# Label-major masks in a graph-attention kernel: contiguous ScalarE copies with strided sums for node tiles 0 and 1, a VectorE multiply-add chain for node tiles 2 and 3

## The chip, the cores and the metric

The kernel runs on one core of one Trainium2 chip. The metric is the device time of one execution in microseconds (us). The core has five engines that each work through a queue of their own in order: TensorE (PE in the profile, with its weight loads as PEld), VectorE (DVE), ScalarE (ACT), GpSimd (POOL) and SyncE (SP), which issues DMA transfers. They wait for each other through semaphores.

## The reference

There are 16 graphs (`B`), each with 512 nodes of 512 features and 11 integer edge labels between every pair of nodes. Two directions of attention are added to a linear layer; only the first 20 nodes are attended to. Cut to what matters here:

```python
adj_f = adj.astype(jnp.float32)                  # (16, 512, 512, 11), entries 0 or 1
self_feat = vcq @ W_self.T + b_self
output = self_feat
for d in range(2):
    A = adj_f if d == 0 else jnp.swapaxes(adj_f, 1, 2)
    A = A[:, :, :20, :]
    cond = A.sum(-1)                             # how many labels an edge has
    vb = A @ w_bias + b_bias                     # the bias of an edge from its labels
    # aff: (16, 512, 16 heads, 20)
    aff = jnp.where(cond[:, :, None, :] > 0, aff, NEG) + vb[:, :, None, :]
    w = jax.nn.softmax(aff, axis=-1)
    output = output + (w applied to the 20 nodes' features, then Wout, bout)
return v + jax.nn.relu(output)
```

The change touches how `cond` (the count over 11 labels) and `vb` (the weighted sum over 11 labels) are formed on the chip. The two together make one additive mask: `vb`, plus -9e15 where the count is zero.

## The kernel before, in words

**Tiling.** A node tile is 128 nodes on the 128 partitions; a graph has 4 of them (`nt` 0 to 3). For each node there are `S` = 40 mask entries (2 directions by 20 nodes) of `L` = 11 labels. Masks are made for two node tiles at a time: `h` = 0 is node tiles 0 and 1, `h` = 1 is node tiles 2 and 3. So one mask step works on 128 partitions by 80 entries by 11 labels = 880 integers, loaded by `load_adj` into `adjs[b, h]`.

**The mask steps.** `mask_mul(b, h)` makes the products label times weight in `prod`, 80 rows of 12 places: on ScalarE by 11 instructions, one per label, that read every 11th integer and write every 12th place (for graph 0 by one ScalarE copy and one GpSimd multiply). `mask_count(b, h)` sums the 11 labels of each entry on VectorE (L323) into `cond`, and GpSimd writes -9e15 or 0 into the 12th place of `prod` (L324). `mask_sum(b, h)` sums the 12 places on VectorE (L329) into `add`. `mask_spread` copies `add` on ScalarE into four partition groups (L338, 16 copies of 32 partitions), and `full_add` on GpSimd (L345) adds the scores' constant part; the result is `full`.

**The loop.** After a setup of some 90 us, each pass of the loop `for b` takes one graph through four node tiles, while the products of the next graph's linear layer are made (`product`, L284, in seven steps after Strassen) and the attention of the previous graph's values is applied (`attend`, L436). For each node tile PE makes the scores (L366); then VectorE does `weigh` (adds the mask L380, takes the maximum L384, subtracts it L388); ScalarE takes the exponential (L393, `expo`); VectorE sums it and takes the reciprocal (`normal`, L416, L417), GpSimd multiplies (L418), and VectorE transposes (`turn`, L425). The softmax of one node tile is finished during the next one.

**The order.** It is written out by hand: each engine's queue holds the instructions in the order of the code. In node tile 0 of graph b stand `mask_mul(b, 1)`, the half of the scores, `normal` of the node tile before, `partial(b, 1, 0)` (L290, which PE's second half of the scores needs), `mask_count(b, 1)`, `joined` (L300), `mask_sum(b, 1)`, half of `mask_spread(b, 1)`, `weigh`, `expo` and the other half. In node tile 2 stands `mask_mul(b + 1, 0)`. In node tile 3 stand `mask_count(b + 1, 0)`, `normal`, `mask_sum(b + 1, 0)`, all of `mask_spread(b + 1, 0)`, then `weigh` and `expo`. So on ScalarE the exponential of node tile 3 stands behind 16 copies that wait for `mask_sum(b + 1, 0)`. `partial(b, f, l)` and `joined(b, key, f, l)` read PE's product out of PSUM and free the bank for the next product. `load_adj(b + 1, 0)` is issued on SP behind `mask_sum(b, 1)` (`done["masks"]`).

Of the kernel before, what the change touches and what calls it, by code (L numbers as in the profile page):

```python
# [7 lines left out]
F32 = mybir.dt.float32  # L8
I32 = mybir.dt.int32
AF = mybir.ActivationFunctionType  # L10
ALU = mybir.AluOpType
AX = mybir.AxisListType

P = 128
NEG = -9000000000000000.0
# [3 lines left out]
def gat_kernel(  # L19
# [19 lines left out]
):  # L39
    nc = tc.nc  # L40
    B, F, N = xT.shape
    NG, L = adj.shape[3], adj.shape[4]
    H, DH = 16, 32
    C = F // P
    HL = P // DH
# [2 lines left out]
    S = 2 * NG  # L48
# [13 lines left out]
    msk = ctx.enter_context(tc.tile_pool(name="msk", bufs=2))  # L62
# [14 lines left out]
    wb_sb = const.tile([P, L], F32, name="wb_sb")  # L77
# [14 lines left out]
    xs, xns, rss, adjs, nzs, sfs, cqs, gs, vds = {}, {}, {}, {}, {}, {}, {}, {}, {}  # L92
    adds, fulls, wts, outs, held, conds, prods = {}, {}, {}, [], [None] * 3, {}, {}
    sums, parts, done, cleared = {}, {}, {}, []


    def behind(one, other):

        if other is not None:
            info = mybir.DependencyInfo(mybir.DependencyClass.Sync, mybir.DependencyReason.DATA)  # L100
            tc.add_manual_dep(one.ins, other.ins.name, info, reason="loads in turn")
# [13 lines left out]
    def load_adj(b, h, ins=None, ts=slice(0, 2)):  # L115
        if ts.start == 0:
            adjs[b, h] = load.tile([P, 2, S * L], I32, tag="adj", name=f"adj{b}_{h}", bufs=3)
        a = adj[b, h * 2 * P : (h + 1) * 2 * P].rearrange("(t p) d m l -> p t (d m l)", p=P)
        behind(nc.sync.dma_start(adjs[b, h][:, ts], a[:, ts]), ins)

    def load_cq(b, ins=None):
# [182 lines left out]
    def new_self(b):  # L304
        sfs[b] = sfp.tile([P, C, N], F32, tag="sf", name=f"sf{b}")
        nc.scalar.copy(sfs[b][:, :, :NG], kvn[:, :, bass.ts(b, NG)])

    def mask_mul(b, h):
        a = adjs[b, h].rearrange("p t (m l) -> p (t m) l", l=L)
        p = prods[b, h] = (msk if h == 0 or b == 0 else xsum).tile(  # L310
            [P, 2 * S, L + 1], F32, tag="prod", name=f"prod{b}_{h}", bufs=1
        )
        if b == 0:
            nc.scalar.copy(p[:, :, :L], a)
            nc.gpsimd.tensor_mul(p[:, :, :L], p[:, :, :L], wb_sb.unsqueeze(1).to_broadcast([P, 2 * S, L]))
        else:
            for l in range(L):
                nc.scalar.activation(p[:, :, l], a[:, :, l], AF.Identity, scale=wb_sb[:, l : l + 1])  # L318

    def mask_count(b, h):  # L320
        a = adjs[b, h]
        cond = msk.tile([P, 2 * S], F32, tag="cond", name=f"cond{b}_{h}")
        nc.vector.tensor_reduce(cond, a.rearrange("p t (m l) -> p (t m) l", l=L), AX.X, ALU.add)  # L323
        nc.gpsimd.tensor_scalar(prods[b, h][:, :, L], cond, 0.0, NEG, ALU.is_le, ALU.mult)  # L324

    def mask_sum(b, h):

        add = conds[b, h] = msk.tile([P, 2 * S], F32, tag="add", name=f"add{b}_{h}")
        done["masks"] = nc.vector.tensor_reduce(add, prods.pop((b, h)), AX.X, ALU.add)  # L329
        adds[b, h] = msk.tile([P, 2, HL, S], F32, tag="both", name=f"both{b}_{h}")  # L330

    def mask_spread(b, h, quarters=range(4)):
# [128 lines left out]
    with tc.tile_pool(name="setup", bufs=1) as sp, tc.tile_pool(name="ps_acc", bufs=4, space=PSUM) as acc["pool"]:  # L461
# [19 lines left out]
        with tc.tile_pool(name="setup_k", bufs=1) as sk:  # L481
# [41 lines left out]
            load_x(0)  # L523
            nc.sync.dma_start(wb_sb, w_bias.partition_broadcast(P))
            load_adj(0, 0)
            nc.sync.dma_start(bq_sb, bq)
            nc.sync.dma_start(bb_sb, b_bias.partition_broadcast(P))
            nc.sync.dma_start(bo_sb, bout)
            for d in range(2):
                rows(wo_sb[:, d], woT[d])  # L530
            load_x(1)
            load_adj(0, 1)


# [90 lines left out]
        with tc.tile_pool(name="setup_g", bufs=3) as sg:  # L625
# [131 lines left out]
            for n, runs in enumerate(bursts):  # L757
# [7 lines left out]
                if rest:  # L765
                    for kind in "mm" if n else ():
                        f, args = steps[kind].pop(0)
# [3 lines left out]
                for kind in plan[n - first] if n - first < len(plan) else ():  # L771
                    f, args = steps[kind].pop(0)
# [3 lines left out]
                if n == 7:  # L776
                    mask_mul(0, 0)
                if n == 8:
                    mask_count(0, 0)
                if n == 10:  # L780
                    mask_sum(0, 0)
                    load_cq(0)
# [13 lines left out]
                if n == 14:  # L796
                    mask_mul(0, 1)
                if n == 15:
                    mask_count(0, 1)
# [10 lines left out]
    with tc.manual_schedule():  # L810
# [10 lines left out]
        for b in range(B):  # L821
# [7 lines left out]
            for nt in range(NT):  # L829
# [13 lines left out]
                if nt == 0:  # L843
                    if b == 0:
                        for g in range(2):
                            scores(b, nt, g, ps[g])
                        mask_sum(b, 1)
                    else:
                        mask_mul(b, 1)
                        product(b, 4)  # L850
                        for g in range(2):
                            scores(b, nt, g, ps[g], range(2))
                        normal(*prev)
                        partial(b, 1, 0)
                        if more:
                            load_x(b + 1, range(2, 3), done["sum"])
                            load_x(b + 1, range(3, C), done["normal"])
                        for g in range(2):
                            scores(b, nt, g, ps[g], range(2, C))
                        if more:  # L860
                            row_mask(b + 1)
                        mask_count(b, 1)
                        joined(b, "c", 1, 1)
                        product(b, 3)
                        load_values(b - 1, done["joined"])
                        mask_sum(b, 1)
                        if more:
                            load_adj(b + 1, 0, done["masks"], slice(0, 1))
                        if b in (3, 4, 5):
                            copies = copies or blocks(1)  # L870
                            spill(1)
# [162 lines left out]
        b = B - 1  # L1034
# [77 lines left out]
```

## Time and profile before

| | |
|---|---|
| three runs | 580.94, 581.45, 582.77 us; median 581.45 us |
| the profiled execution's span, first to last instruction | 578.9 us |
| the median less that span (what lies around it) | 2.55 us |
| busy: PE, PEld, DVE, ACT, POOL | 99%, 75%, 85%, 68%, 70% |
| granted PE clock over the span | 0.998 |
| one pass of the loop in the steady state | 30.48 us |

No separate time is listed for the profiled execution; its span stands for it, and the difference to the median of the runs is kept as what lies around it. Lines of the profile give start, length, engine, line of the kernel, operation, output and inputs, and in brackets how long the engine sat idle before and whom it waited for. A group of several instructions ("x11") is given from the start of the first to the end of the last.

### The profile page before, as it was taken

To read this page: it belongs to the slowest core of one execution; us is meant where nothing else is said; L and a number is where in the kernel's file an instruction comes from. 1 tells how busy PE (TensorE), PEld (TensorE's weight loads), DVE (VectorE), ACT (ScalarE), POOL (GpSimd) and SP (SyncE) were. 2 spreads that over 40 slices of the span, in tenths; PEclk is the share of its full clock that TensorE was granted. 3 is DMA by queue.
4 is the path that set the end of the run, shared out by engine and by line. 5 is a ranking of instruction groups with operands and counts; after the bars stand their busy time and mean duration, and the time that the engine had idled before them with its cause. 6 is when DMAs were issued, how large, how long until landed. Compare 5 with 4: busy or idle time off the path is not lost.

```text
span 578.9 us, 31006 instructions
## 1 busy us (share of the span) xinstructions
PE 572.2 (99%) x13508; PEld 434.1 (75%) x13508; DVE 492.9 (85%) x790; ACT 393.6 (68%) x1162; POOL 404.6 (70%) x383
## 2 busy tenths in 40 slices
PE   9999999999999999999999999999999999999996
PEld 6544458888878787878778787877887878787873
DVE  0675776979898989898999999898989898989896
ACT  1234554687878777778786868687887877777571
POOL 2726986658586776858585867776858677785874
PEclk9999999999999999999999999999999999999999
DMA  8998997867777767777676777566666766674404
GB/s 315 382 396 283 333 361 233 237 195 219 209 233 185 220 187 204 213 185 228 167 220 166 222 166 220 164 206 180 204 193 192 195 192 189 192 208 111 147 19 147
DMA packets 98788, 123.26 MB, mean 213 GB/s; under 512 B 18877, under 2 KB 66969, under 8 KB 96605
## 3 DMA queue, kind: packets, MB, share of 16 engines
q1 hardware_dynamic: 96268, 117.54, 67.8%
q0 software_dynamic: 1392, 2.43, 1.8%
q8 instruction: 106, 1.74, 1.3%
q10 hardware_dynamic: 992, 1.31, 0.6%
q14 instruction: 30, 0.24, 0.1%
HBM read 82.30 MB, written 40.24 MB: 212 GB/s over the span
## 4 chain that ended last, share of the span: by engine, by line
PE 98%; DVE 1%; issue 0%; DVEq 0%
PE ps_s L366 46%; PE ps_a L284 19%; PE ps_c L284 9%; PE ps_o L436 6%; PE ps_d L284 5%; PE ps_v L658 3%; PE ps_k L598 3%; PE ps_kv L541 1%; PE ps_o L813 1%; PE ps_warm L500 1%; PE ps_nz L214 0%; PE ps_s L355 0%; PE _g(2, 2, 0, 14, 16)0_845 L692 0%; PE _g(0, 2, 0, 14, 16)0_448 L692 0%; PE g(3, 2, 0, 14, 16)0_1055 L692 0%
## 5 line engine op out<-in xcount | busy, mean ns | idle before, releaser
L366 PEld LDWEIGHTS ps_s<-g,sf 128*32 128x32 f32 x8192 | 263.6, 110 | 21.9 <-issue 14.8
L366 PE MATMUL ps_s<-g,sf 128*32 128x152 f32 x8192 | 278.1, 293 | 0.7 <-issue 0.7
L338 ACT COPY both<-add 32x80 f32<-32x80 f32 x512 | 130.9, 256 | 60.9 <-DVE add L329 55.1
L418 POOL TENSOR_TENSOR s<-s,sm 128x640 f32<-128x640 f32 x63 | 80.4, 1275 | 96.8 <-DVE sm L417 52.5
L345 POOL TENSOR_TENSOR full<-cq,both 128x640 f32<-128x640 f32 x64 | 100.3, 1568 | 26.9 <-issue 20.9
L318 ACT ACTIVATE prod<-adj,wb_sb 128x80 f32<-128x80 int32 x330 | 112.4, 432 | 0.0
L393 ACT ACTIVATE s<-s 128x640 f32<-128x640 f32 x63 | 46.5, 738 | 56.0 <-DVE s L388 55.6
L450 POOL TENSOR_TENSOR o<-o,x 128x512 f32<-128x512 f32 x60 | 76.3, 1293 | 0.0
L380 DVE TENSOR_TENSOR full<-ps_s,full 128x608 f32<-128x608 f32 x63 | 48.6, 772 | 22.5 <-PE ps_s L366 19.4
L284 PE MATMUL ps_a<-t,ws_s 128*32 128x246 f32 x1024 | 59.8, 371 | 0.0
L416 DVE TENSOR_REDUCE sm<-s 128x32 f32<-128x640 f32 x63 | 50.8, 807 | 10.5 <-ACT s L393 10.3
L384 DVE TENSOR_REDUCE ps_s<-full 128x32 f32<-128x640 f32 x63 | 52.2, 828 | 2.2
L425 DVE STREAM_TRANSPOSE wt<-s 128x640 f32<-128x640 f32 x63 | 52.8, 838 | 0.6 <-POOL s L418 0.6
L388 DVE TENSOR_TENSOR s<-full,ps_s 128x640 f32<-128x640 f32 x63 | 51.5, 818 | 1.1
L290 DVE SCALAR_TENSOR_TENSOR sf<-nz,qw,ps_a 128x246 f32<-128x246 f32 x128 | 51.5, 443 | 0.1
L284 PEld LDWEIGHTS ps_a<-t,ws_s 128*32 128x32 f32 x1024 | 34.4, 110 | 16.8 <-issue 0.8
L329 DVE TENSOR_REDUCE add<-prod 128x80 f32<-128x960 f32 x32 | 36.8, 1150 | 7.4 <-ACT prod L318 4.0
L447 ACT ACTIVATE o<-o,bo 128x512 f32<-128x512 f32 x60 | 38.3, 713 | 0.6 <-DVE o L445 0.6
L249 POOL TENSOR_TENSOR t<-x,t 128x492 f32<-128x492 f32 x32 | 36.8, 1151 | 1.3
L436 PE MATMUL ps_o<-wt,vd 32*32 32x512 f32 (+5 forms) x816 | 36.9, 578 | 0.0
L249 POOL TENSOR_TENSOR t<-x 128x492 f32<-128x492 f32 x32 | 36.8, 1151 | 0.0
L445 DVE TENSOR_TENSOR o<-ps_o,sf 128x512 f32<-128x512 f32 x60 | 36.7, 668 | 0.0
(225 smaller groups left out, 715.8 us busy)
## 6 DMA issues: line engine op xcount, KB each, us to landing
g<-g_d SPq DMA_DIRECT2D x60, 304.0 KB
g_d<-st SPq DMA_DIRECT2D x16, 1064.0 KB
out_T<-o SPq DMA_DIRECT2D x60, 256.0 KB
xn<-in_xn SPq DMA_DIRECT2D x56, 256.0 KB
x<-in_xT SPq DMA_DIRECT2D x56, 256.0 KB
adj<-in_adj SPq DMA_DIRECT2D x60, 220.0 KB
nz<-nz_d SPq DMA_DIRECT2D x14, 256.0 KB
wk<-in_wkT SPq DMA_DIRECT2D x2, 1024.0 KB
```

The costliest lines, as they stand in the source:

```text
L249: done["xsum"] = nc.gpsimd.tensor_sub(t, one, two)
L284: nc.tensor.matmul(to, lhs, x[:, k], start=start, stop=stop, skip_group_check=n != 2)
L290: done["partial"] = nc.vector.scalar_tensor_tensor(to[:, i], nzs[b][:, half(l)], qw[:, 2 * f + i, b : b + 1], parts[b, "a"][i][:, :HN], AL ...
L318: nc.scalar.activation(p[:, :, l], a[:, :, l], AF.Identity, scale=wb_sb[:, l : l + 1])
L338: done["spread"] = nc.scalar.copy(adds[b, h][bass.ts(a, R), :, g], add[r].rearrange("p (t m) -> p t m", t=2))
L345: done["full"] = nc.gpsimd.tensor_add(f, cqs[b].unsqueeze(1).to_broadcast(shape), adds[b, nt // 2][:, nt % 2].unsqueeze(2).to_broadcast(sh ...
L366: nc.tensor.matmul(to, sfs[b][:, k, bass.ds(nt * P + (2 * g + j) * R, R)], of, start=(onto is None and k == 0 and (whole or j == 0)), stop ...
L384: nc.vector.tensor_reduce(mx, f, AX.X, ALU.max)
L418: done["normal"] = nc.gpsimd.tensor_mul(s, s, sm.unsqueeze(3).to_broadcast(full))
L425: nc.vector.transpose(wts[b][:, nt], s.rearrange("p a h m -> p (a h m)"))
L436: nc.tensor.matmul(banks[a][bass.ds(at // 2 * DH, n * DH)].rearrange("p (t n) -> p t n", n=32), vd[r, bass.ds(at * DH, n * DH)], wt[r, :, ...
L450: nc.gpsimd.tensor_add(o[:, c], o[:, c], xs[b][:, c])
```

## The change

The integers come in label-major: for each node tile 11 runs of 40 entries in place of 40 runs of 11 labels. The host transposes them (outside the measured time), the bytes per transfer are the same. The product tile becomes 12 rows of 80 places.

- `mask_mul(b, 0)`: 11 ScalarE instructions as before, now with contiguous runs of 40 in and 80 out, for graph 0 too (its ScalarE copy and GpSimd multiply are gone).
- `mask_mul(b, 1)`: nothing is computed; only the tile is allocated.
- `mask_count(b, h)`: the same count on VectorE, but its 11 inputs for each entry stand 40 places apart. The GpSimd step writes a contiguous row.
- `mask_sum(b, 0)`: the same sum on VectorE, with its 12 inputs 80 places apart.
- `mask_sum(b, 1)`: in place of the sum, 11 VectorE multiply-adds of 80 elements, each adding label times weight to the result of the one before, starting from the -9e15 row.

```diff
     def mask_mul(b, h):
-        a = adjs[b, h].rearrange("p t (m l) -> p (t m) l", l=L)
         p = prods[b, h] = (msk if h == 0 or b == 0 else xsum).tile(
-            [P, 2 * S, L + 1], F32, tag="prod", name=f"prod{b}_{h}", bufs=1
+            [P, L + 1, 2 * S], F32, tag="prod", name=f"prod{b}_{h}", bufs=1
         )
-        if b == 0:
-            nc.scalar.copy(p[:, :, :L], a)
-            nc.gpsimd.tensor_mul(p[:, :, :L], p[:, :, :L], wb_sb.unsqueeze(1).to_broadcast([P, 2 * S, L]))
+        if h == 1:
+            return
+        for l in range(L):
+            nc.scalar.activation(
+                p[:, l].rearrange("p (t m) -> p t m", t=2), labels(b, h)[:, l], AF.Identity, scale=wb_sb[:, l : l + 1]
+            )
+    def labels(b, h):
+        return adjs[b, h].rearrange("p t (l m) -> p l t m", l=L)
...
+    def mask_count(b, h):
+        cond = msk.tile([P, 2, S], F32, tag="cond", name=f"cond{b}_{h}")
+        nc.vector.tensor_reduce(cond, labels(b, h).rearrange("p l t m -> p t m l"), AX.X, ALU.add)
+        nc.gpsimd.tensor_scalar(prods[b, h][:, L], cond.rearrange("p t m -> p (t m)"), 0.0, NEG, ALU.is_le, ALU.mult)
...
     def mask_sum(b, h):
+        if h == 0:
+            done["masks"] = nc.vector.tensor_reduce(add, p.rearrange("p l m -> p m l"), AX.X, ALU.add)
         else:
+            to = add.rearrange("p (t m) -> p t m", t=2)
             for l in range(L):
+                done["masks"] = nc.vector.scalar_tensor_tensor(
+                    to, labels(b, h)[:, l], wb_sb[:, l : l + 1],
+                    to if l else p[:, L].rearrange("p (t m) -> p t m", t=2), ALU.mult, ALU.add,
+                )
```

On VectorE in node tile 0 of a middle graph, before: the count (L323), `joined` (L300), the sum (L329), then `weigh` (L380 to L388).

```order
L323 TENSOR_REDUCE cond_1_4179<-adj_1_3646 128x80
L300 TENSOR_TENSOR sf_3889<-ps_c_4041,sf_3889 128x2x246
L329 TENSOR_REDUCE add_1_4204<-prod_1_4076 128x80
L380 TENSOR_TENSOR full_0_4073<-ps_s_0_4075,full_0_4073 128x32x19
L384 TENSOR_REDUCE ps_s_0_4075<-full_0_4073 128x32
L388 TENSOR_TENSOR s_0_4220<-full_0_4073,ps_s_0_4075 128x640
```

The same place now, with the line numbers of the changed kernel (L324 is the count, L336 the multiply-add, L390 to L398 `weigh`) and with the semaphores that each waits for:

```order
L324 TENSOR_REDUCE cond_1_4181<-adj_1_3659 128x80 [waits DMAHW7_49,DMAHW0_49]
L300 TENSOR_TENSOR sf_3902<-ps_c_4054,sf_3902 128x2x246
L336 SCALAR_TENSOR_TENSOR add_1_4206<-adj_1_3659,wb_sb,prod_1_4089 128x80 [waits Pool_49]
L336 SCALAR_TENSOR_TENSOR add_1_4206<-adj_1_3659,wb_sb,add_1_4206 128x80 [waits DVE_49] x10
L390 TENSOR_TENSOR full_0_4086<-ps_s_0_4088,full_0_4086 128x32x19 [waits PE_49]
```

One instruction became eleven, ten of which wait for the one before; the wait for ScalarE is gone, that for GpSimd stays.

On ScalarE from the masks of `h` = 0 of one graph to the second half of the copies of `h` = 1, before:

```order
L338 COPY both_0_2733<-add_0_2731 32x2x40 x16
L393 ACTIVATE s_3_2852<-s_3_2852 128x640
L318 ACTIVATE prod_1_2866<-adj_1_2437,wb_sb 128x80 x11
L338 COPY both_1_2996<-add_1_2994 32x2x40 x8
L393 ACTIVATE s_0_3010<-s_0_3010 128x640
```

The same place now (the copies are L348, the exponential is L403):

```order
L348 COPY both_0_2748<-add_0_2746 32x2x40 x16
L403 ACTIVATE s_3_2867<-s_3_2867 128x640
L348 COPY both_1_3010<-add_1_2998 32x2x40 x8
L403 ACTIVATE s_0_3024<-s_0_3024 128x640
L348 COPY both_1_3010<-add_1_2998 32x2x40 x8
```

The 11 products of `h` = 1 are gone from ScalarE; the order of what is left is the same, and the 16 copies still stand ahead of the exponential of node tile 3.

More of the change, by code (lines that the diff above doesn't have):

```diff
@@ L41, in gat_kernel @@
     B, F, N = xT.shape
-    NG, L = adj.shape[3], adj.shape[4]
+    L, NG = adj.shape[2], adj.shape[4]
     H, DH = 16, 32
@@ L117, in load_adj @@
             adjs[b, h] = load.tile([P, 2, S * L], I32, tag="adj", name=f"adj{b}_{h}", bufs=3)
-        a = adj[b, h * 2 * P : (h + 1) * 2 * P].rearrange("(t p) d m l -> p t (d m l)", p=P)
+        a = adj[b, h * 2 * P : (h + 1) * 2 * P].rearrange("(t p) l d m -> p t (l d m)", p=P)
         behind(nc.sync.dma_start(adjs[b, h][:, ts], a[:, ts]), ins)
@@ L306, in new_self @@
         nc.scalar.copy(sfs[b][:, :, :NG], kvn[:, :, bass.ts(b, NG)])
+    def labels(b, h):
+        return adjs[b, h].rearrange("p t (l m) -> p l t m", l=L)
     def mask_mul(b, h):
-        a = adjs[b, h].rearrange("p t (m l) -> p (t m) l", l=L)
         p = prods[b, h] = (msk if h == 0 or b == 0 else xsum).tile(
-            [P, 2 * S, L + 1], F32, tag="prod", name=f"prod{b}_{h}", bufs=1
+            [P, L + 1, 2 * S], F32, tag="prod", name=f"prod{b}_{h}", bufs=1
         )
-        if b == 0:
-            nc.scalar.copy(p[:, :, :L], a)
-            nc.gpsimd.tensor_mul(p[:, :, :L], p[:, :, :L], wb_sb.unsqueeze(1).to_broadcast([P, 2 * S, L]))
-        else:
-            for l in range(L):
-                nc.scalar.activation(p[:, :, l], a[:, :, l], AF.Identity, scale=wb_sb[:, l : l + 1])
+        if h == 1:
[4 more added lines that the diff above has]
+            )
@@ L320, in mask_count @@
     def mask_count(b, h):
[L321 to L324, printed above, removed]
+        cond = msk.tile([P, 2, S], F32, tag="cond", name=f"cond{b}_{h}")
+        nc.vector.tensor_reduce(cond, labels(b, h).rearrange("p l t m -> p t m l"), AX.X, ALU.add)
+        nc.gpsimd.tensor_scalar(prods[b, h][:, L], cond.rearrange("p t m -> p (t m)"), 0.0, NEG, ALU.is_le, ALU.mult)
@@ L326, in mask_sum @@
     def mask_sum(b, h):
         add = conds[b, h] = msk.tile([P, 2 * S], F32, tag="add", name=f"add{b}_{h}")
-        done["masks"] = nc.vector.tensor_reduce(add, prods.pop((b, h)), AX.X, ALU.add)
+        p = prods.pop((b, h))
+        if h == 0:
+            done["masks"] = nc.vector.tensor_reduce(add, p.rearrange("p l m -> p m l"), AX.X, ALU.add)
+        else:
+            to = add.rearrange("p (t m) -> p t m", t=2)
+            for l in range(L):
+                done["masks"] = nc.vector.scalar_tensor_tensor(
+                    to, labels(b, h)[:, l], wb_sb[:, l : l + 1],
+                    to if l else p[:, L].rearrange("p (t m) -> p t m", t=2), ALU.mult, ALU.add,
+                )
@@ L1087 @@
         "qT": chunked(given["cond_1024"]).transpose(0, 2, 1),
-        "adj": np.stack([mask[:, :, :NG], mask[:, :NG].transpose(0, 2, 1, 3)], axis=2),
+        "adj": np.stack([mask[:, :, :NG], mask[:, :NG].transpose(0, 2, 1, 3)], axis=2).transpose(0, 1, 4, 2, 3),
         "wsT": w["W_self"].T,
```

## The prediction

> **What bounds the kernel now.** I read the page first: who is busy, and what the chain that ended last consists of.
>
> ```profile
> span 578.9 us, 31006 instructions
> ...
> PE 572.2 (99%) x13508; PEld 434.1 (75%) x13508; DVE 492.9 (85%) x790; ACT 393.6 (68%) x1162; POOL 404.6 (70%) x383
> ...
> PE 98%; DVE 1%; issue 0%; DVEq 0%
> ```
>
> TensorE (PE) is busy for 572.2 of 578.9 us and makes up 98% of the chain: it is the bound, and nothing the change does makes PE's work shorter. The most that can be won is PE's idle 6.7 us. What can be lost depends on how much room VectorE (DVE) has, since the change gives it more work. So I took one pass of the loop in the middle by the busy-time windows (columns: length, busy PE, PEld, DVE, ACT, POOL, clock, DMA), from one sum L416 of node tile 3 to the next:
>
> ```profile
> 301.17:331.65 30.48, 30.48 (x792) 24.21 (x784) 27.83 (x43) 23.48 (x72) 22.04 (x20) 1.00 0.70 195
> ```
>
> PE fills the pass of 30.48 us without a gap; DVE has 2.65 us of it free. Where that freedom lies, DVE's timeline of the pass shows:
>
> ```profile
> 301.17 0.82 DVE L416 TENSOR_REDUCE sm<-s 128x32 f32<-128x640 f32 x1 [0.57 <-ACT s L393]
> 302.02 0.35 DVE L417 RECIPROCAL sm<-sm 128x32 f32<-128x32 f32 x1
> ...
> 302.96 1.06 DVE L323 TENSOR_REDUCE cond<-adj 128x80 f32<-128x880 int32 x1
> 303.94 0.66 DVE L300 TENSOR_TENSOR sf<-ps_c,sf 128x492 f32<-128x492 f32 x1
> 304.89 1.16 DVE L329 TENSOR_REDUCE add<-prod 128x80 f32<-128x960 f32 x1 [0.29 <-ACT prod L318]
> 305.96 0.78 DVE L380 TENSOR_TENSOR full<-ps_s,full 128x608 f32<-128x608 f32 x1
> ...
> 311.69 0.79 DVE L380 TENSOR_TENSOR full<-ps_s,full 128x608 f32<-128x608 f32 x1 [0.81 <-PE ps_s L366]
> ...
> 319.85 0.84 DVE L290 SCALAR_TENSOR_TENSOR sf<-nz,qw,ps_a 128x246 f32<-128x246 f32 x2
> ...
> 325.41 1.15 DVE L329 TENSOR_REDUCE add<-prod 128x80 f32<-128x960 f32 x1
> ...
> 331.65 0.82 DVE L416 TENSOR_REDUCE sm<-s 128x32 f32<-128x640 f32 x1 [0.58 <-ACT s L393]
> ```
>
> From the sum L416 at 301.17 to the end of the mask sum at 326.56 (25.39 us) DVE waits only twice: 0.29 and 0.81 us. What follows is not DVE's alone. ScalarE (ACT) makes 16 copies of that mask sum before it gets to the exponential that the next L416 needs:
>
> ```profile
> 326.59 4.27 ACT L338 COPY both<-add 32x80 f32<-32x80 f32 x16 [1.88 <-DVE add L329]
> 330.88 0.74 ACT L393 ACTIVATE s<-s 128x640 f32<-128x640 f32 x1
> ```
>
> So there is a ring in every pass: DVE from L416 to the mask sum, then 326.56 to 331.65 (5.09 us) on ACT, then L416 again. Without its two waits the ring takes 25.39 - 1.10 + 5.09 = 29.38 us against PE's 30.48. **The slack is 1.10 us per pass.** What DVE gets in addition beyond it lengthens each pass; the rest of DVE's free time lies beside the copies and the exponential on ACT and cannot be used. PE can't run ahead of this ring: its product behind the scores waits in every pass for DVE's L290 (319.85, done at 320.69), which stands between two of `weigh`'s steps, with only 0.44 us to spare:
>
> ```profile
> 321.13 1.85 PE L284 MATMUL ps_a<-t,ws_s 128*32 128x246 f32 x32
> ```
>
> **The change part by part.** The chain of multiply-adds. What it replaces takes 1.07 us in the order (304.89 to the next start at 305.96). For a scalar_tensor_tensor on data in SBUF the trace has one group:
>
> ```profile
> L611 DVE SCALAR_TENSOR_TENSOR bqt<-wq_sb,br_sb 128x512 f32<-128x512 f32 x8 | 5.4, 715 | 0.0
> L318 ACT ACTIVATE prod<-adj,wb_sb 128x80 f32<-128x80 int32 x330 | 112.4, 432 | 0.0
> L338 ACT COPY both<-add 32x80 f32<-32x80 f32 x512 | 130.9, 256 | 60.9 <-DVE add L329 55.1
> L314 ACT CAST prod<-adj 128x880 f32<-128x880 int32 x2 | 1.9, 926 | 0.0
> L323 DVE TENSOR_REDUCE cond<-adj 128x80 f32<-128x880 int32 x32 | 33.5, 1046 | 0.0
> L329 DVE TENSOR_REDUCE add<-prod 128x80 f32<-128x960 f32 x32 | 36.8, 1150 | 7.4 <-ACT prod L318 4.0 <-POOL t L249 2.8 <-POOL prod L324 0.6
> ```
>
> A contiguous element costs DVE 1.06 ns (L416 takes 0.82 us for 640, L329 1.16 for 960). L611's fixed part is then 715 - 512 x 1.06 = 172 ns, and 80 elements take 85 + 172 = 0.26 us (the runs of 40 are contiguous). Each link waits for the link before. Such a pair is in the timeline: L416 ends at 301.99, the reciprocal that needs it starts at 302.02, 30 ns later (independent neighbours overlap: L323 ends at 304.02, the next starts at 303.94). So a link is 0.29 us, eleven are 3.19, less 0.08 by which an independent successor overlaps: 3.11 us, and **+2.04 us** against 1.07. Bounds: links that overlap like independent neighbours, 0.18 us each, +0.91; with a gap twice as long, +2.4. The Trainium skill ("VectorE: DVE Perf Modes", section "The DRAIN you can't avoid") says that a semaphore after each of eight copies costs nothing against one at the end; by that the links would take 0.18 us and the chain +0.91. The trace disagrees, by 30 ns of gap where independent neighbours overlap by 80; I take 0.29.
>
> The strided sums. Both counts of a pass and the sum of `h` = 0 now step 40 and 80 words between neighbours. The trace of before has no DVE instruction that reads so. The nearest rows are ACT's products L318, which read and write at 11 and 12 words, beside the contiguous copies L338 of the same size. In the timeline of ACT, 11 products took 3.74 us and 8 copies 2.14 (the first row is graph 1's, used below):
>
> ```profile
> 119.59 3.75 ACT L318 ACTIVATE prod<-adj,wb_sb 128x80 f32<-128x80 int32 x11
> ...
> 301.04 3.74 ACT L318 ACTIVATE prod<-adj,wb_sb 128x80 f32<-128x80 int32 x11
> 306.08 2.14 ACT L338 COPY both<-add 32x80 f32<-32x80 f32 x8 [1.29 <-DVE add L329]
> ```
>
> From start to start that is (3.74 - 0.432)/10 = 0.331 and (2.14 - 0.256)/7 = 0.269 us: 62 ns for 80 elements, **0.77 ns per element**. Bounds: 0, if DVE's reads don't mind, and 2.2, if the whole difference of the durations (432 - 256) is the stride's. I take 0.77, since start to start is what an engine in order pays. Each count then costs 880 x 0.77 = 0.68 us more, the sum of `h` = 0 960 x 0.77 = 0.74.
>
> The skill speaks against the change here: "Vector Engine (DVE) Microarchitecture Reference", section 5.2 "Measured stream behaviour on trn2", has 1.73 ns per column for a source that hops at every element against 1.05 for contiguous ones. By that 0.68 ns the sum below would be +41.0 and the time 622 us; no run shows it on DVE yet.
>
> What leaves ACT (11 products of `h` = 1, 3.74 us per pass) lies beside PE: ACT then waited 1.29 us for DVE in any case. What comes first on ACT now is the same wait for `add`, and the 16 copies in the ring are untouched. `h` = 0's products become contiguous, likely cheaper, and nothing waits for them. Loads: `load_adj` behind `done["masks"]` goes out some 2 us later on SP, and with it what stands behind it there; its first reader is `mask_mul(b + 1, 0)`, two node tiles later. GpSimd's -9e15 row is still waited for by the first link; it ran beside L300, and any rest is below 0.2 us.
>
> **Sum.** Per pass: two counts 1.36, the sum 0.74, the chain 2.04, together 4.14 us. The ring takes 29.38 + 4.14 = 33.52 us, **3.04 us** above PE's 30.48. The ends:
>
> ```profile
> 117.27 0.82 DVE L416 TENSOR_REDUCE sm<-s 128x32 f32<-128x640 f32 x1 [0.49 <-ACT s L393]
> ...
> 123.45 1.15 DVE L329 TENSOR_REDUCE add<-prod 128x80 f32<-128x960 f32 x1 [2.76 <-POOL t L249]
> ...
> 554.05 0.82 DVE L416 TENSOR_REDUCE sm<-s 128x32 f32<-128x640 f32 x1 [0.47 <-ACT s L393]
> ```
>
> From L416 at 117.27, graph 0's, to graph 14's there are 14 passes. In 13 of them 3.04 us: 39.5. The first has a wait of 2.76 us that goes (the row names POOL, but ACT's products, above, end at 123.34, just ahead of 123.45): 4.14 - 2.76 = 1.4. Ahead of it, graph 0's pass has one count and one sum more in the ring: 0.68 + 0.74 = 1.4. Behind it, graph 15 has one count and the chain, 2.72, less waits of 0.29 (as in the middle pass) and 0.47: 2.0. In the setup ACT gets 11 products (11 x 0.269 = 3.0 us) in place of one conversion (L314, 0.93 us), GpSimd loses a multiply; I take 0.5, between 0 and 2. Together 44.8 us on the span: 623.7, and with the 2.55 us around it **626.3 us** (the median 581.45 + 44.8).
>
> **The rivals.**
> - *Strides are free on DVE.* A read stream of one source may keep its full rate. For it: no DVE row speaks against it, and ACT's rows have a strided write too. Then only the chain is left: +2.04 per pass, 0.94 beyond the slack; 13 x 0.94 = 12.2, 1.3 at the end and 0.5 in the setup make 14.0, **595 us**. The same section of the skill has this as an exception: a one-source op that hops every element was measured at the full rate.
> - *Steep strides.* At 1.5 ns per element, half-way between 0.77 and 2.2: 1.32 per count, 1.44 for the sum, 6.12 per pass; 13 x 5.02 + 3.4 + 2.8 + 2.6 + 0.5 = 74.6, **656 us**. The section has this as well: 2.5 ns for steps of 24 words.
> - *Hidden, not slower.* The links overlap like independent neighbours (0.18 us each, +0.91) and strides are free: less than 1.10 us per pass, so PE hides all and the time stays at **581.5 us**. The point is the slack: with contiguous rates it decides at (1.10 + 1.07)/11 = 0.197 us per link. Against it stand the 30 ns gap and the 0.26 us. A gain would have to come from the setup, where GpSimd's multiply goes: at most a part of the 6.7 us of PE's idle, say 579.
>
> **How the numbers follow.** The forecast gets 0.57, free strides 0.20, steep strides 0.15, hidden 0.05, a gain 0.03. About 0.3% (1.7 us) is what a measurement of this kernel can tell from no change. The first three are slower by more: 0.92. The range goes from free strides with a little less in the chain (594) into the steep case (652); it leaves out hidden, gain and over half of the steep case, some 0.17.
>
> **What would show it right or wrong.** Right: L336 appears 16 x 11 times with some 0.26 us each and 0.29 from start to start; the counts (L324) take 1.7 us in place of 1.05, the sums of `h` = 0 (L332) 1.9 in place of 1.15; the pass is 33.5 us, with PE idle in it about 3 us and waiting for DVE; DVE idles only ahead of L426 behind ACT's exponential. Wrong: counts of 1.05 us with a pass near 31.4 (free strides), counts above 2.2 us (steep), a pass still at 30.5 (hidden), or PE waiting for something other than DVE.

## The result, and the profile after

The changed kernel takes 672.56 us (median of 4 runs, 671.92 to 673.86) against 581.42 us: 1.157 times as long, 95% interval 1.154 to 1.160. The forecast was 626.3 us with a range up to 652. The sign was right; the loss is 91 us where 45 was forecast.

The page of the changed kernel, with the lines that answer to those of before:

```profile
span 670.3 us, 30996 instructions
...
PE 605.3 (90%) x13508; PEld 444.6 (66%) x13508; DVE 593.9 (89%) x950; ACT 326.6 (49%) x1006; POOL 398.5 (59%) x381
...
PEclk9999999999898999899999989899989989899989
...
PE 42%; DVE 34%; ACT 11%; issue 10%; POOL 1%; DMA 1%; POOLq 0%; DVEq 0%; ACTq 0%
```

PE's share of the chain that ended last falls from 98% to 42%; DVE has 34% of it and ACT 11%, the ring of the prediction. PE's granted clock, 9 tenths or more in every slice of before, is 8 in some; its mean over the span goes from 0.998 to 0.971. DVE's busy time rose by 101 us, though its new instructions were to cost some 66 (16 x 4.14). What they cost singly stands in the groups (output and inputs, count, busy us and mean ns of one, idle time before):

```profile
L336 DVE SCALAR_TENSOR_TENSOR add<-adj,wb_sb,add 128x80 f32<-128x80 int32 x160 | 58.5, 365 | 5.7
L324 DVE TENSOR_REDUCE cond<-adj 128x80 f32<-128x880 int32 x32 | 58.4, 1826 | 0.0
L332 DVE TENSOR_REDUCE add<-prod 128x80 f32<-128x960 f32 x16 | 29.3, 1831 | 0.0
L336 DVE SCALAR_TENSOR_TENSOR add<-adj,wb_sb,prod 128x80 f32<-128x80 int32 x16 | 27.4, 1710 | 0.5
```

The strided sums came out as forecast: a count 1.83 us (forecast 1.7, before 1.05), the sum of `h` = 0 1.83 (1.9, before 1.15). The links did not: the first of each chain lasts 1.71 us in the mean, the ten others 0.365. DVE's timeline of a pass in the middle shows which:

```profile
340.23 0.82 DVE L426 TENSOR_REDUCE sm<-s 128x32 f32<-128x640 f32 x1 [1.30 <-ACT s L403]
...
342.03 1.82 DVE L324 TENSOR_REDUCE cond<-adj 128x80 f32<-128x880 int32 x1
343.76 0.67 DVE L300 TENSOR_TENSOR sf<-ps_c,sf 128x492 f32<-128x492 f32 x1
344.46 1.70 DVE L336 SCALAR_TENSOR_TENSOR add<-adj,wb_sb,prod 128x80 f32<-128x80 int32 x1
346.20 0.98 DVE L336 SCALAR_TENSOR_TENSOR add<-adj,wb_sb,add 128x80 f32<-128x80 int32 x1
...
347.21 0.30 DVE L336 SCALAR_TENSOR_TENSOR add<-adj,wb_sb,add 128x80 f32<-128x80 int32 x1
347.55 0.30 DVE L336 SCALAR_TENSOR_TENSOR add<-adj,wb_sb,add 128x80 f32<-128x80 int32 x1
...
350.13 0.78 DVE L390 TENSOR_TENSOR full<-ps_s,full 128x608 f32<-128x608 f32 x1
...
376.36 0.82 DVE L426 TENSOR_REDUCE sm<-s 128x32 f32<-128x640 f32 x1 [1.30 <-ACT s L403]
```

The chain takes 344.46 to 350.13, 5.67 us in place of the 3.11 forecast. Two links are long, and GpSimd's timeline beside them says what runs meanwhile:

```profile
343.94 0.49 POOL L325 TENSOR_SCALAR prod<-cond 128x80 f32<-128x80 f32 x1 [0.87 <-DVE cond L324]
344.51 1.56 POOL L355 TENSOR_TENSOR full<-cq,both 128x640 f32<-128x640 f32 x1
346.02 1.05 POOL L249 TENSOR_TENSOR t<-x 128x492 f32<-128x492 f32 x1
```

`full_add` (L355) ends at 346.07, the first link at 346.16; `x_sum` (L249) ends at 347.07, the second link at 347.18. From then on GpSimd is idle and each link takes 0.30 us. A link has two inputs in SBUF; it seems to stand still until the GpSimd instruction beside it has ended. The pass is 36.13 us here; of the 14 passes four are 36.1 us and ten 36.4 to 36.8. Where the 91.4 us of the span lie, the first and the last L426 of node tile 3 tell; before, the first stood at 117.27 and the last was this row (the prediction's row at 554.05 is node tile 0 of the graph after; its count of 14 passes is right):

```profile
544.99 0.82 DVE L416 TENSOR_REDUCE sm<-s 128x32 f32<-128x640 f32 x1 [0.57 <-ACT s L393]
```

Now, in DVE's timeline of the changed kernel:

```profile
120.61 0.82 DVE L426 TENSOR_REDUCE sm<-s 128x32 f32<-128x640 f32 x1 [1.35 <-ACT s L403]
...
631.88 0.82 DVE L426 TENSOR_REDUCE sm<-s 128x32 f32<-128x640 f32 x1 [1.29 <-ACT s L403]
```

3.3 us ahead of the first (forecast 1.9), 83.6 us in the 14 passes (511.3 in place of 427.7; forecast 40.9), 4.5 behind (forecast 2.0).

### The profile page after: what moved, and what is told of

Read it like the earlier page. It is cut to its first block, busy times and chain, and to the rows that moved or that the text cites. A ratio compares the mean times of both kernels' runs of the same rounds, so it can differ in the third digit from the quotient of the medians.

```text
span 670.3 us, 30996 instructions
## 1 busy us (share of the span) xinstructions
PE 605.3 (90%) x13508; PEld 444.6 (66%) x13508; DVE 593.9 (89%) x950; ACT 326.6 (49%) x1006; POOL 398.5 (59%) x381
## 4 chain that ended last, share of the span: by engine, by line
PE 42%; DVE 34%; ACT 11%; issue 10%; POOL 1%; DMA 1%; POOLq 0%; DVEq 0%; ACTq 0%
PE ps_s L376 17%; ACT both L348 9%; PE ps_o L446 7%; DVE cond L324 7%; DVE sm L426 4%; DVE sf L290 4%; DVE add L332 4%; PE ps_a L284 4%; PE ps_c L284 4%; DVE add L336 3%; DVE wt L435 3%; DVE sf L300 3%; PE ps_k L608 3%; PE ps_v L668 2%; ACT s L403 2%
## 5 line engine op out<-in xcount | busy, mean ns | idle before, releaser
L376 PE MATMUL ps_s<-g,sf 128*32 128x152 f32 x8192 | 286.6, 295 | 7.5 <-DVE sf L290 6.2
L348 ACT COPY both<-add 32x80 f32<-32x80 f32 x512 | 130.8, 256 | 217.0 <-DVE add L336 155.9
L428 POOL TENSOR_TENSOR s<-s,sm 128x640 f32<-128x640 f32 x63 | 80.3, 1274 | 146.3 <-DMA nz<-nz_d 73.1
L355 POOL TENSOR_TENSOR full<-cq,both 128x640 f32<-128x640 f32 x64 | 100.0, 1562 | 47.9 <-issue 41.3
L446 PE MATMUL ps_o<-wt,vd 32*32 32x512 f32 (+5 forms) x816 | 56.8, 789 | 43.9 <-issue 43.9
L403 ACT ACTIVATE s<-s 128x640 f32<-128x640 f32 x63 | 46.5, 737 | 58.4 <-DVE s L398 58.0
L426 DVE TENSOR_REDUCE sm<-s 128x32 f32<-128x640 f32 x63 | 50.9, 808 | 21.1 <-ACT s L403 20.9
L336 DVE SCALAR_TENSOR_TENSOR add<-adj,wb_sb,add 128x80 f32<-128x80 int32 x160 | 58.5, 365 | 5.7
L446 PEld LDWEIGHTS ps_o<-wt,vd 32*32 32x32 f32 (+1 forms) x816 | 14.5, 129 | 69.8 <-issue 66.7
L324 DVE TENSOR_REDUCE cond<-adj 128x80 f32<-128x880 int32 x32 | 58.4, 1826 | 0.0
L398 DVE TENSOR_TENSOR s<-full,ps_s 128x640 f32<-128x640 f32 x63 | 51.5, 818 | 1.1
L390 DVE TENSOR_TENSOR full<-ps_s,full 128x608 f32<-128x608 f32 x63 | 48.2, 765 | 4.1 <-PE ps_s L376 3.9
L284 PEld LDWEIGHTS ps_a<-t,ws_s 128*32 128x32 f32 x1024 | 37.7, 110 | 14.7 <-issue 2.6
L318 ACT ACTIVATE prod<-adj,wb_sb 128x80 f32<-128x80 int32 x176 | 45.9, 347 | 0.0
L249 POOL TENSOR_TENSOR t<-x,t 128x492 f32<-128x492 f32 x32 | 36.8, 1151 | 1.3
```

The lines of the kernel that those rows point to most:

```text
L284: nc.tensor.matmul(to, lhs, x[:, k], start=start, stop=stop, skip_group_check=n != 2)
L324: nc.vector.tensor_reduce(cond, labels(b, h).rearrange("p l t m -> p t m l"), AX.X, ALU.add)
L336: done["masks"] = nc.vector.scalar_tensor_tensor(to, labels(b, h)[:, l], wb_sb[:, l : l + 1], to if l else p[:, L].rearrange("p (t m) -> p ...
L348: done["spread"] = nc.scalar.copy(adds[b, h][bass.ts(a, R), :, g], add[r].rearrange("p (t m) -> p t m", t=2))
L355: done["full"] = nc.gpsimd.tensor_add(f, cqs[b].unsqueeze(1).to_broadcast(shape), adds[b, nt // 2][:, nt % 2].unsqueeze(2).to_broadcast(sh ...
L376: nc.tensor.matmul(to, sfs[b][:, k, bass.ds(nt * P + (2 * g + j) * R, R)], of, start=(onto is None and k == 0 and (whole or j == 0)), stop ...
```

## The experiments

**Theory A**: a DVE instruction with two SBUF inputs is held by a GpSimd tensor operation. **Theory B**: the first link is long of itself. The first run tells these apart; the three after it take away one part of the change each.

### GpSimd later

`behind(x, y)` makes x wait for y.

```diff
                     full_add(b, 1)
+                    behind(done["full"], done["masks"])
```

> The changed kernel, with GpSimd's full_add(b, 1) made to wait for the last link of the chain (x_sum(b + 1, 1) stands behind it), so that GpSimd is idle while VectorE runs the chain. Theory A (a VectorE instruction with two SBUF inputs stands still while a GpSimd tensor operation runs): the first link falls from 1.70 to about 0.30 us, the second from 0.98 to 0.30, the chain from 5.67 to about 3.7 us, the pass from 36.1-36.8 to about 34.2 us, the gap of 3.0 us ahead of attend to about 1; time about 637 us. Theory B (the first link is long of itself: it is the first to read the row that GpSimd wrote): the first link stays at 1.7 us and the time at 672 us or a little above, since GpSimd is later.

635.56 us, 1.094 times before (1.089 to 1.099). The links in the groups and in DVE's timeline of this kernel:

```profile
L336 DVE SCALAR_TENSOR_TENSOR add<-adj,wb_sb,prod 128x80 f32<-128x80 int32 x16 | 4.8, 301 | 0.5
```

```profile
329.35 0.30 DVE L336 SCALAR_TENSOR_TENSOR add<-adj,wb_sb,prod 128x80 f32<-128x80 int32 x1
329.68 3.34 DVE L336 SCALAR_TENSOR_TENSOR add<-adj,wb_sb,add 128x80 f32<-128x80 int32 x10
332.94 0.78 DVE L390 TENSOR_TENSOR full<-ps_s,full 128x608 f32<-128x608 f32 x1
```

The first link, 1.71 us before, takes 0.30; the chain 3.59. Nothing on DVE was changed, only when GpSimd runs. All passes are 34.0 to 34.1 us. Theory B is out. The Trainium skill has the rule ("SBUF — State Buffer", section "SBUF: two separate sides"): DVE and GpSimd share a pair of SBUF ports, whoever starts first holds it for the whole instruction, and a DVE instruction with two SBUF inputs needs it. The trace agrees in the hold, with 1.70 against 0.30 us. Who starts first it does not show: the row of the held first link starts at 344.46, 0.05 us ahead of the row of `full_add` at 344.51.

### Sums only, and chain only

The layout without the chain:

```diff
-        if h == 1:
-            return
         for l in range(L):
...
-        if h == 0:
+        if True:
             done["masks"] = nc.vector.tensor_reduce(add, p.rearrange("p l m -> p m l"), AX.X, ALU.add)
```

> The label-major layout without the chain: node tiles 2 and 3 are made as 0 and 1 are, by 11 contiguous ScalarE products and a strided sum. Theory A: per pass two counts at +0.78 and two sums at +0.69 us, 2.94 less the slack of 1.10: a pass of 32.3 us, time about 609 us, no VectorE instruction held by GpSimd. If the strided sums were the main cost and the chain a small one, the time would stay above 650 us.

607.60 us, 1.046 (1.042 to 1.050); twelve of 14 passes are 32.1 to 32.2 us, the first is 33.2 and one 32.4. As expected, so two strided counts and two strided sums per pass cost some 28 us over the 580.0 us of before beside it.

The chain with `h` = 0 as before the change; the host leaves the first 256 nodes of each graph entry-major:

```diff
...
+        if h == 0:
+            cond = msk.tile([P, 2 * S], F32, tag="cond", name=f"cond{b}_{h}")
+            nc.vector.tensor_reduce(cond, adjs[b, h].rearrange("p t (m l) -> p (t m) l", l=L), AX.X, ALU.add)
+            nc.gpsimd.tensor_scalar(prods[b, h][:, :, L], cond, 0.0, NEG, ALU.is_le, ALU.mult)
+            return
...
```

> Node tiles 0 and 1 as before the change (entry-major, strided ScalarE products, contiguous count and sum), node tiles 2 and 3 label-major with the chain and one strided count. Theory A: per pass the count at +0.78 and the chain at +4.6 us, 5.38 less the slack of 1.10: a pass of 34.8 us plus some 0.4 where PE's clock falls, time about 648 us. If the strided sums were the main cost, about 600 us.

649.63 us, 1.119 (1.114 to 1.123); passes 34.6 to 35.4 us. The larger part of the loss hangs on the chain (this kernel keeps one strided count per pass).

### Contiguous reads, alone and with GpSimd later

```diff
-        nc.vector.tensor_reduce(cond, labels(b, h).rearrange("p l t m -> p t m l"), AX.X, ALU.add)
+        nc.vector.tensor_reduce(cond.rearrange("p t m -> p (t m)"), adjs[b, h].rearrange("p t (m l) -> p (t m) l", l=L), AX.X, ALU.add)
...
-            done["masks"] = nc.vector.tensor_reduce(add, p.rearrange("p l m -> p m l"), AX.X, ALU.add)
+            done["masks"] = nc.vector.tensor_reduce(add, p.rearrange("p l m -> p (l m)").rearrange("p (m l) -> p m l", l=L + 1), AX.X, ALU.add)
```

> The changed kernel with the counts and the sum of node tiles 0 and 1 reading the same 880 and 960 places in their order in memory, so that they add up other places than they should; everything else as changed. This takes away the strides alone. The counts go back to about 1.05 us, the sum to 1.15 us: 2 x 0.78 + 0.69 = 2.25 us less per pass, a pass of about 34.1 us, time about 640 us. If strides cost more than their own instructions show (by holding others), the time falls further.

637.33 us, 1.097 (1.092 to 1.101); passes 33.9 to 34.5 us. The counts and the sum are back to their old prices, in the groups of this kernel:

```profile
L324 DVE TENSOR_REDUCE cond<-adj 128x80 f32<-128x880 int32 x32 | 33.5, 1045 | 0.0
L332 DVE TENSOR_REDUCE add<-prod 128x80 f32<-128x960 f32 x16 | 18.3, 1146 | 0.0
```

So the stride alone costs 1826 - 1045 = 781 ns for 880 elements (0.89 ns each, 40 words apart) and 1831 - 1146 = 685 ns for 960 (0.71 ns each, 80 apart).

> Contiguous reads for the counts and the sum of node tiles 0 and 1 (they add up other places than they should) and GpSimd's full_add(b, 1) behind the chain, both at once. What is left is the chain alone, 11 links of 0.335 us = 3.7 us in place of 1.07. Theory A: the effects add up, 34.05 - 2.25 = 31.8 us per pass, time about 602 us. If the two effects are one (strides hold GpSimd and so the links), the time stays near 635 us.

601.86 us, 1.037 (1.035 to 1.040), each pass 31.8 us: the two effects add up, 34.05 - 31.80 = 2.25 us per pass for the strides.

### Two accumulators

On the kernel with GpSimd later:

```diff
-            to = add.rearrange("p (t m) -> p t m", t=2)
...
+            to = [add.rearrange("p (t m) -> p t m", t=2), p[:, 0].rearrange("p (t m) -> p t m", t=2)]
+            nc.vector.scalar_tensor_tensor(
+                to[0], labels(b, h)[:, 0], wb_sb[:, 0:1], p[:, L].rearrange("p (t m) -> p t m", t=2), ALU.mult, ALU.add,
+            )
+            nc.vector.tensor_scalar(to[1], labels(b, h)[:, 1], wb_sb[:, 1:2], None, ALU.mult)
+            for l in range(2, L):
+                nc.vector.scalar_tensor_tensor(
+                    to[l % 2], labels(b, h)[:, l], wb_sb[:, l : l + 1], to[l % 2], ALU.mult, ALU.add,
                 )
+            done["masks"] = nc.vector.tensor_add(add, add, p[:, 0])
...
```

> The kernel with GpSimd later, and the chain split onto two accumulators in turn, 12 instructions, each waiting for the one before the last; the last adds the two. If the wait of a link for the link before costs what the prediction took (30 ns of gap and 80 ns of lost overlap), start to start falls from 0.335 to about 0.18-0.2 us, the chain from 3.7 to about 2.4 us, the pass from 34.05 to 32.8, time about 617 us. If a wait costs nothing, start to start stays at 0.335, twelve make 4.0 us and the time is about 640 us.

619.77 us, 1.069 (1.067 to 1.072). DVE's timeline of this kernel, three links in a row:

```profile
322.36 0.30 DVE L340 SCALAR_TENSOR_TENSOR prod<-adj,wb_sb,prod 128x80 f32<-128x80 int32 x1
322.57 0.30 DVE L340 SCALAR_TENSOR_TENSOR add<-adj,wb_sb,add 128x80 f32<-128x80 int32 x1
322.78 0.30 DVE L340 SCALAR_TENSOR_TENSOR prod<-adj,wb_sb,prod 128x80 f32<-128x80 int32 x1
```

Start to start is 0.21 us where the single chain has 0.34 (347.21 to 347.55), though each link still needs the result of the link before the last. Needing the direct predecessor costs 0.13 us per link; the passes fall from 34.05 to 33.05.

### Accumulating in PSUM

GpSimd where it was, but only one input of each multiply-add in SBUF:

```diff
-            to = add.rearrange("p (t m) -> p t m", t=2)
...
+            to = pair[:, 1, 384 : 384 + 2 * S].rearrange("p (t m) -> p t m", t=2)
+            nc.vector.tensor_scalar(to, labels(b, h)[:, 0], wb_sb[:, 0:1], None, ALU.mult)
+            for l in range(1, L):
+                nc.vector.scalar_tensor_tensor(
+                    to, labels(b, h)[:, l], wb_sb[:, l : l + 1], to, ALU.mult, ALU.add,
                 )
+            done["masks"] = nc.vector.tensor_add(
+                add.rearrange("p (t m) -> p t m", t=2), to, p[:, L].rearrange("p (t m) -> p t m", t=2)
+            )
...
```

> The changed kernel, GpSimd where it was, but the chain accumulates in a free piece of PSUM: a first multiply (one input), ten multiply-adds with one input in SBUF and one in PSUM, and a last add of the -9e15 row into SBUF. Theory A (only two SBUF inputs are held by GpSimd): no instruction of the chain lasts over 0.45 us, twelve make about 4.2 us in place of 5.67, a pass of about 34.7 us, time about 645 us. If any VectorE instruction is held while GpSimd runs a tensor operation, the first two last 1.7 and 1.0 us as before and the time is 672 us or more.

643.36 us, 1.109 (1.107 to 1.112); passes 34.3 us. The group of the links in this kernel, then the links of one pass and what GpSimd runs beside them:

```profile
L337 DVE SCALAR_TENSOR_TENSOR ps_s<-adj,wb_sb,ps_s 128x80 f32<-128x80 int32 x160 | 49.0, 306 | 5.7
```

```profile
334.14 3.38 DVE L337 SCALAR_TENSOR_TENSOR ps_s<-adj,wb_sb,ps_s 128x80 f32<-128x80 int32 x10
333.97 1.55 POOL L358 TENSOR_TENSOR full<-cq,both 128x640 f32<-128x640 f32 x1
335.48 1.05 POOL L249 TENSOR_TENSOR t<-x 128x492 f32<-128x492 f32 x1
```

The same two GpSimd operations run beside the links, and no link is held, at the price of one instruction more. This confirms theory A from the other side: DVE as such is not held. The links' output moved to PSUM together with their second input; that the output is not what is held, the count of the changed kernel shows: at 342.03 it has one input in SBUF, writes to SBUF and ran beside GpSimd's L428 (341.58 to 342.85), and took 1.82 us, as long as all others.

### Step of 20 words

```diff
     def labels(b, h):
-        return adjs[b, h].rearrange("p t (l m) -> p l t m", l=L)
+        return adjs[b, h].rearrange("p t (d l m) -> p l (t d) m", d=2, l=L)
```

> The changed kernel with the labels laid out for each direction apart: runs of 20, so that the count's 11 inputs stand 20 words apart in place of 40; the sum of node tiles 0 and 1 keeps its 80 words. If any hop costs the same, the count stays at 1.83 us; if short steps cost more (40 words cost 0.89 ns per element, 80 words 0.71), it rises above 2.0 us and the time to 680 us or more.

The expectation was wrong: the count takes less, and yet the one run took 686.07 us (no interval). The group, the window over an attend (columns as in the prediction; the clock stands ahead of the DMA share), and DVE's timeline behind it:

```profile
L324 DVE TENSOR_REDUCE cond<-adj 128x80 f32<-128x880 int32 x32 | 55.8, 1744 | 0.0
```

```profile
358.70:363.30 4.60, 4.54 (x52) 1.21 (x56) 4.50 (x7) 2.59 (x10) 2.84 (x3) 0.50 0.38 98
```

```profile
368.37 0.79 DVE L390 TENSOR_TENSOR full<-ps_s,full 128x608 f32<-128x608 f32 x1 [1.43 <-POOL s L428]
```

Behind a wait of PE of 3 us the granted clock is 0.50; attend takes 4.46 us, the scores behind it (363.15 to 368.22) end late, and DVE's L390, which reads them, starts 1.43 us late (the row names GpSimd, but L390 reads PE's scores). All passes here but the first are 37.5 to 37.6 us. The same in the changed kernel, in a pass of 36.56 us, with DVE's L390 behind it:

```profile
389.60:393.70 4.10, 4.09 (x53) 1.20 (x57) 4.00 (x7) 2.10 (x9) 2.38 (x3) 0.59 0.39 90
```

```profile
398.04 0.79 DVE L390 TENSOR_TENSOR full<-ps_s,full 128x608 f32<-128x608 f32 x1 [0.26 <-PE ps_s L376]
```

In the changed kernel's four passes of 36.1 us attend takes 2.70 us at a granted clock of 1.00, and this L390 waits for nothing; in the ten others attend takes 3.6 to 4.2 us at 0.58 to 0.73, and in nine of them L390 waits 0.15 to 0.57 us for PE's scores.

### PE kept busy

Were the uneven passes of the changed kernel an effect of PE's clock, or did the clock only go with them? **Theory C**: the clock falls because PE waits, and the slower scores then delay DVE.

```diff
                     for g in range(2):
                         scores(b, nt, g, ps[g])
+                    if b > 0:
+                        for _ in range(18):
+                            nc.tensor.matmul(pair[:, 1, 384:512], ident, ident, start=True, stop=True, skip_group_check=True)
```

> The changed kernel with 18 multiplications of an unused 128 x 128 identity into an unused piece of PSUM, between the scores of node tile 1 and attend in graphs 1 to 15, some 2.5 us of the 3.0 us in which PE waits there. VectorE's work is untouched. Theory C (PE's granted clock falls because PE idles for 3 us there, and what follows at the lower clock then delays VectorE): the clock is 1.00 in every attend, attend takes 2.7 us or less in all passes, all passes are about 36.1 us, the time falls by some 5 to 6 us to about 667 us. Theory D (the passes of 36.5 to 36.8 us have another cause, and the clock only goes with it): passes stay uneven, time 672 us or, if the added work delays something, more.

665.48 us, 1.146 (1.144 to 1.148), 7.1 us less than the changed kernel by adding work to PE (6.4 us of it in the 14 passes). The added multiplications take 4.29 us where some 2.5 were expected, so PE has no gap at all ahead of attend. The window over an attend of this kernel, and the same attend in PE's timeline:

```profile
387.62:389.86 2.24, 2.24 (x53) 0.59 (x56) 2.14 (x5) 0.94 (x4) 1.67 (x2) 1.00 0.31 84
```

```profile
387.62 2.24 PE L446 MATMUL ps_o<-wt,vd 32*64 32x512 f32 x48
```

All passes are 36.0 to 36.1 us, the length of the changed kernel's four short ones, and the mean clock of the span is 1.000. Theory C holds.

## Why the prediction was right or wrong

**The bound and the ring were right.** The ring of DVE, 16 copies and the exponential sets the pass, and DVE's one wait in the pass shown is 1.30 us ahead of L426 behind ACT. With both side effects undone the pass is 31.80 us; the forecast's formula with the measured chain gives 29.38 + 3.59 - 1.07 = 31.90.

**The strides were sized right**, in part by luck: 0.89 and 0.71 ns per element were measured, and the 0.77 came from another engine at steps of 11 and 12 words; one was above it and one below, and the pass pays 2.25 us where 2.10 were forecast. The rival of steep strides, whose 656 us is nearest to the result, is not what happened.

**The step that failed is the chain**, +2.04 us per pass in the sum, measured as 5.67 - 1.07 = +4.60. Two things were mis-sized. A link without disturbance is 0.335 us from start to start, not 0.29: eleven make 0.5 us per pass (the gap of 30 ns was right, but the link itself lasts 0.30 us and not 0.26). And the sum priced a link from L611, which also has two SBUF inputs but mostly no GpSimd tensor operation beside it, and so put the influence of GpSimd's work at nothing; that costs 2.0 us per pass. The trace of before had the row that speaks against it, in the setup, in the timelines of DVE and GpSimd put together by time:

```profile
17.89 0.48 DVE L583 TENSOR_TENSOR kvD<-kvn 128x304 f32<-128x304 f32 x1
18.00 1.52 POOL L223 TENSOR_TENSOR ws_s<-ws_v 128x512 f32<-128x512 f32 x1
...
18.80 1.05 DVE L583 TENSOR_TENSOR kvD<-kvn 128x304 f32<-128x304 f32 x1
19.60 1.40 POOL L224 TENSOR_TENSOR ws_s<-ws_s,ws_v 128x512 f32<-128x512 f32 x1
...
20.29 1.04 DVE L583 TENSOR_TENSOR kvD<-kvn 128x304 f32<-128x304 f32 x1
```

L583, with two SBUF inputs of 304 elements, takes 0.48 us and then 1.05 and 1.04, and the two long ones end 0.33 us after a GpSimd instruction ended (19.52 to 19.85, 21.00 to 21.33). None of DVE's instructions in the loop of before has two SBUF inputs, so its rows in the loop couldn't show the hold.

**A second thing was not in the sum**: that PE, once it waits for 3 us, goes on at a lower clock in most passes, and that this comes back to DVE as a wait; that is the 7.1 us of the last experiment.

The account in times: 672.6 (changed) - 7.1 (PE's clock, 665.5) - 29.9 (GpSimd's hold, 635.6) - 33.7 (strides, 601.9) leaves some 21 us over before, mostly the chain itself beyond the slack (1.32 us in each of the 14 passes). The kernel before took 579.6 to 581.4 us beside these runs, so each term is good to some 2 us. The forecast's 626.3 with links of 0.335 us (about 7 us) and the strides as measured (about 2) would have come to some 635 us; the kernel in which GpSimd doesn't disturb took 635.6. The ends took some 4 us more than forecast: behind the last pass the 4.5 us fall to 2.7 with GpSimd later; ahead of the first, 1.8 us stay with contiguous reads and GpSimd later, where the setup was put at 0.5. Of the variants that form the same masks, the one without the chain is the fastest, 607.6 us, and it too is slower than before.

**What stays open**: which of the two engines has to start first for the link to be held; why attend takes 2.70 us behind a gap of 0.93 us and 2.24 without one, both at a granted clock of 1.00; why 20 words between inputs cost less (0.79 ns) than 40 and more than 80; each distance is one point, and 80 words were measured on floats.

## What to carry to other kernels

Before pricing a new VectorE instruction from another row, compare where its inputs lie: with two inputs in SBUF it stood still here until the GpSimd tensor operation beside it had ended, so it is priced with GpSimd's timeline beside it; moving GpSimd's operation, or keeping one input in PSUM, took the hold away. A chain in which each link needs the last pays for that at every link; two chains in turn took a link from 0.34 to 0.21 us from start to start. And when a change makes TensorE wait in every pass, here for 3 us, what it does next may run at a lower clock; that is an addition to the wait.

## What the runs showed of the hardware

- **The hold**: a link of 0.30 us took 1.70 and 0.98 us beside GpSimd operations of 1.56 and 1.05, ending 0.09 and 0.11 us after them; with one input in PSUM a link took 0.306 us beside the same operations, and DVE's sums with one SBUF input were not held (the count at 342.03 ran for 1.82 us beside GpSimd's multiply, as long as all others).
- **PE's clock**: with GpSimd later, PE's gap ahead of attend is 0.93 us, the clock over the run was 0.998 and attend took 2.70 us in every pass; in the changed kernel, after gaps of 2.6 to 3.0 us, it was 2.70 us in four passes and 3.6 to 4.2 in ten, with 0.58 to 0.73 granted. The Trainium skill ("TensorE: Matmul & The Clock Gate", section "Part 1: The HAM clock gate (the "warmup" mystery)") has a window of about 3.4 us that runs freely, after which an idle PE falls to half its clock. The trace agrees in the 0.50 granted with the step of 20 words, and in that equal gaps differ from pass to pass, as they would against a window that runs freely. It does not agree in the length: the gaps here are shorter than that window, and the clock fell all the same.
- **Dependent links**: needing the direct predecessor cost 0.13 us per link against needing the one before it.
